# Four convolution-like layers on one core: query blocks of 10 rows in the attention layer, and three changes around it

## The chip, the core and the metric

The kernel runs on one core of a Trainium2 chip. The core has five engines with a queue of instructions each: TensorE (PE in the profile, with its weight loads as PEld), VectorE (DVE), ScalarE (ACT), GpSimd (POOL) and SyncE (SP, which here only issues DMAs). An engine takes its own instructions in the order in which they stand, and waits on semaphores for what other engines make. Data lie in SBUF (128 partitions), sums of matmuls in PSUM (eight banks), the rest in DRAM. The metric is the device time of one execution in microseconds (us); lower is better.

## What is computed

Four layers run one after the other on 4 images of 256 channels and 48 x 48 points, each as x = x + layer(norm(x)), all in float32. Layer 0 is a dilated 7 x 7 convolution whose softmax weights mix shifted copies of x. Layer 1 is a 3 x 3 convolution with signs for weights, layer 2 a 3 x 3 convolution with ternary weights (their size compared with 0.7 of its mean). Layer 3 is a linear attention with three windows, cut to what matters:

```python
q = sigmoid(Wq x); k = sigmoid(Wk x); v = Wv x / |Wv x|     # 8 heads of 32 channels
for w in (1, 2, 4):                # window of 48, 24, 12 points a side
    wkv  = box(integral(k v^T))    # sum over the window around each point
    wk   = box(integral(k))
    outs.append((q . wkv) / (q . wk + 1e-6))
x = x + Wout concat(outs) + bout
```

The kernel computes layer 3 in another order: scores q.k for all pairs of points within the widest window, times a mask of 0 and 1 for each window, times v.

## The kernel before

**Layers 0 to 2** (up to line 1440) run image by image. For image b the order on the queues is `attend(b)` (softmax and mixing of layer 0), `layer1`, `layer2`, `prelude(b + 2)`. Matmuls of the next image's convolution, `conv0(b + 1)`, are a *filler*: a generator from which `fill(us)` draws pieces where TensorE would otherwise wait. A second generator, `side`, prepares the weights of layers 1 and 2 once, during image 0: each `fill` also takes one step of it, and what is left after `attend(0)` is drained at lines 1430 and 1431, one step per `fill(1)`. `prepare_layer1` (line 577) loads a group of weights, takes signs on ScalarE, stores them; `prepare_layer2` (line 595) sums sizes with 18 matmuls (`abs_ps`), then for six groups loads again, takes size and sign on ScalarE, compares on VectorE (`kept`) and sums with 72 thin matmuls (`sum_ps`). For the last image the filler is `project_first` (line 1406), which makes q, k and v of image 0 in 12 groups for layer 3.

**Layer 3** (from line 1442) goes through blocks `(b, ct, rb)`: image, half of the channels (4 heads), query rows. A block before has 8 rows (RB, 384 points), so 6 to an image, 48 in all. Keys come in tiles of 8 rows by 16 columns: (a, c), with a from 0 to 5 and c from 0 to 2. Per tile:

- `scores` (1656): TensorE makes s = k.q for 4 heads in two pairs, a pair to a PSUM tile of two banks. The pool holds two such tiles, so one key tile fills it.
- `masked` (1674): `full` (1715) tells whether the widest window covers the middle columns for the whole block. If so, ScalarE copies these columns, and VectorE multiplies only the edges by the mask; if not, VectorE multiplies everything (`widest`). If the narrowest window is seen too (`many`), VectorE also makes the middle window from PSUM (`middle`), and GpSimd the narrowest from SBUF.
- `sums` (1767): TensorE multiplies by v into three accumulators, two tiles later (LAG = 2). So the order on TensorE is s(n), sums(n-2), s(n+1), sums(n-1).

`tiles_of` (1789) sets tiles with the narrow window (here *near*) and the others in alternation. The others are *ring* tiles (full, but not near) and *far* tiles (not full).

After each tile `advance()` takes a step of the jobs in the background: `Projection` of the next image (one part every two steps), `k_sums` (1491) and `norms` (1533) in a chain, which make the denominators on VectorE and GpSimd, and `finish` (1830), which divides and applies Wout (`out_ps`). A job's `yield n` puts its next step n tiles later; FETCH is 4. `until(key)` takes steps on the spot until something is made. `norms` loads `nhi` and `nlo` for both halves at once, then takes difference and product for one half after the other on GpSimd, sums on TensorE (`norm_ps`) and stores reciprocals (`r_d`). `prepare` (1803) loads them spread over partitions (`rc`). Keys and values have 12 buffers each (`kvp`, line 1445), and `LOADS` (1887) says after which block which key rows of the next half are loaded. All layer 3 loads go over SP's queue, at the start too: four pairs of key and value tiles, then q (lines 1881 to 1884). The masks come over GpSimd's queue (line 1458).

Most instructions carry line 142, that of the helper which records them; so they are told apart by the names of their tiles.

Of the kernel before, what the change touches and what calls it, by code (L numbers as in the profile page):

```python
# [21 lines left out]
P = 128  # L22
B, C, H, W = 4, 256, 48, 48
HW = H * W
# [56 lines left out]
NKT = NRB * NKC  # L81

# [63 lines left out]
def conv_preact_kernel(  # L146
# [76 lines left out]
    o_d = [dram.tile([NRB, P, NW * NB], F32, tag=f"o{b}", name=f"o_d{b}") for b in range(B)]  # L223
    n_d = [dram.tile([NRB, HEADS, NW, NB], F32, tag=f"n{b}", name=f"n_d{b}") for b in range(B)]
    r_d = [dram.tile([NRB, HEADS, NW, NB], F32, tag=f"r{b}", name=f"r_d{b}") for b in range(B)]
# [61 lines left out]
    class Projection:  # L287
# [6 lines left out]

        def ps_tile(self):
            t = self.psum.tile(self.shape, F32, tag=self.tag, name="proj_ps")
            return t if len(self.shape) == 2 else t[:, 0]

        def load(self, g, a, n):

            b = self.b
            yield from take("xr")
            xr = self.scr.tile([P, NCT, RB, W], F32, tag="xr", name="xr")
            sync.dma_start(
                out=xr,
                in_=x3_d[b][:, a * RB : (a + 1) * RB, :].rearrange(
                    "(ct p) r w -> p ct r w", p=P
                ),
            )
            yield FETCH  # L310
            yield from take("xn")
            xn = self.scr.tile([P, NCT, NKC, P], F32, tag="xn", name="xn")
            for ct in range(NCT):
                dve.tensor_scalar(
                    xn[:, ct].rearrange("p c (r x) -> p c r x", x=KC),
                    xr[:, ct].rearrange("p r (c x) -> p c r x", x=KC),
                    st3[:, b, 0, ct : ct + 1],
                    st3[:, b, 1, ct : ct + 1],
                    ALU.subtract,
                    ALU.mult,  # L320
                )
                yield 1
            free["xr"] += 1
            self.xn[g], self.uses[g] = xn, n
# [7 lines left out]
        def qk(self, g, a, name, mo):  # L332
            b = self.b
            while g not in self.xn:
                yield 1
# [29 lines left out]
        def v(self, g, a, c):  # L365
            b = self.b
            while g not in self.xn or (c > 0 and g not in self.vs):
                yield 1
# [74 lines left out]
    with (  # L443
# [133 lines left out]
        def prepare_layer1():  # L577
            for ct in range(NCT):
                for g in range(T1 // 3):
                    raw = new_wl().rearrange("p a o -> p (a o)")[:, 0 : 3 * C]  # L580
                    raw = raw.rearrange("p (t o) -> p t o", t=3)
                    sync.dma_start(out=raw, in_=wl1[ct * P : (ct + 1) * P, 3 * g : 3 * g + 3, :])
                    signs = new_wl().bitcast(BF16).rearrange("p a o -> p (a o)")[:, 0 : 3 * C]
                    signs = signs.rearrange("p (t o) -> p t o", t=3)
                    act.activation(signs, raw, AF.Sign)
                    for mo in range(NCT):
                        sync.dma_start(
                            out=wl1_d[mo, :, ct, 3 * g : 3 * g + 3, :],
                            in_=signs[:, :, mo * P : (mo + 1) * P],
                        )  # L590
                    yield
# [3 lines left out]
        def prepare_layer2():  # L595
# [14 lines left out]
            loaded = [load_raw(*groups[0])]  # L610
            for i, (ct, g) in enumerate(groups):
                if i + 1 < len(groups):
                    loaded.append(load_raw(*groups[i + 1]))
# [3 lines left out]
                for t in range(3):  # L617
# [6 lines left out]
                    )  # L624
            delta = smx.tile([P, 1, C], F32, tag="delta", name="delta", bufs=1)
# [10 lines left out]
            for i, (ct, g) in enumerate(groups):  # L636
                both = new_wl().rearrange("p (a t) o -> p a (t o)", a=2)
                both = both.rearrange("p a (t o) -> p a t o", t=3)
                signs, size = both[:, 0], both[:, 1]
                kept = new()  # L640
                sync.dma_start(out=signs, in_=wl2[ct * P : (ct + 1) * P, 3 * g : 3 * g + 3, :])
                rows.append(both)
                yield
# [7 lines left out]
                for what, src in ((0, size), (1, kept)):  # L651
                    for mo in range(NCT):
                        for t in range(3):
# [3 lines left out]
                                ones[:, 0:1],  # L657
# [367 lines left out]
        def apply0(xt, k, rows_at_hand, load_next, xTs):  # L1025
# [24 lines left out]
            for f in range(NPH):  # L1050
                now = seen
# [135 lines left out]
        def layer2(b, stats):  # L1187
# [70 lines left out]
            for h in range(thirds):  # L1258
                for mo in range(NCT):
                    for at in range(N2):  # L1260
                        ps = ps_cv.tile([P, R2, W], F32, tag="cv3", name="cv3")
# [130 lines left out]
        with (  # L1392
# [13 lines left out]
            def project_first():  # L1406
# [10 lines left out]
                start(paced(Projection(0, scr, ps, "ps", [P, 512]).groups(groups), 1))  # L1417
# [4 lines left out]
            for b in range(B):  # L1422
                if b + 1 < B:
                    filler = conv0(b + 1, {})
                else:
                    ending.close()
                    wts3 = ctx.enter_context(tc.tile_pool(name="wts_qkv", bufs=1, side="right"))
                    filler = project_first()
                stats = attend(b)
                for _ in side:  # L1430
                    fill(1)
# [11 lines left out]
    with (  # L1443
        tc.tile_pool(name="wts3", bufs=1, reuse_waits="tile") as wts,
        tc.tile_pool(name="kvp", bufs=2 * NRB, reuse_waits="tile") as kvp,
# [12 lines left out]
        masks = wts.tile([P, NMASK], BF16, name="masks")  # L1458
        nc.gpsimd.dma_start(out=masks, in_=masks_in[:, 0:NMASK])
# [9 lines left out]
        zeros = wts.tile([P, NB], BF16, name="zeros")  # L1469
# [63 lines left out]
        def norms(b, rb):  # L1533
# [4 lines left out]
            def load(ct):  # L1538
                chans = slice(ct * P, (ct + 1) * P)
                hi = scr.tile([P, NW, RB, W], F32, tag="nhi", name="nhi")  # L1540
                lo = scr.tile([P, NW, RB, W], F32, tag="nlo", name="nlo")
# [5 lines left out]
                for wi, h in enumerate(HALVES):  # L1547
# [7 lines left out]
                    if n < RB:  # L1555
# [3 lines left out]
                        )  # L1559

                    y0 = rb * RB - h - 1
# [5 lines left out]
                return hi, lo, qf  # L1567
# [5 lines left out]
            loaded = [load(ct) for ct in range(NCT)]  # L1573
            yield FETCH
            for hi, lo, qf in loaded:
                for wi, h in enumerate(HALVES):
                    n = min(RB, max(0, h + 1 - rb * RB))
                    if n < RB:
                        pool.tensor_sub(hi[:, wi, n:RB], hi[:, wi, n:RB], lo[:, wi, n:RB])
                yield 1  # L1580
# [22 lines left out]
            nn = HEADS * NW * NB // P  # L1603
            nr = scr.tile([P, nn], F32, tag="nr", name="nr")
            flat = [d[b][rb].rearrange("h w n -> (h w n)") for d in (n_d, r_d)]
            sync.dma_start(out=nr, in_=flat[0].rearrange("(p n) -> p n", n=nn))
# [4 lines left out]
            sync.dma_start(out=flat[1].rearrange("(p n) -> p n", n=nn), in_=nr)  # L1611
# [13 lines left out]
        def load_q(b, ct, rb):  # L1625
            qs = qp.tile([P, RB, W], F32, tag="qs", name="qs")
            sync.dma_start(
                out=qs.rearrange("p r w -> p (r w)"),
                in_=q_d[b][ct * P : (ct + 1) * P, rb * NB : (rb + 1) * NB],
# [3 lines left out]
        def rows_seen(wi, a, rb):  # L1633

            h = HALVES[wi]
            return (
                max(0, a * RB - h + 1 - rb * RB),
                min(RB, a * RB + RB + h - rb * RB),
            )
# [5 lines left out]
        class Block:  # L1645


            def __init__(self, b, ct, rb, qs):
# [5 lines left out]
                self.accs = self.stage = None  # L1654

# [18 lines left out]
            def masked(self, a, c, ss):  # L1674
# [8 lines left out]
                            [P, 2, RB, min(W, KC + 2 * HALVES[wi])],  # L1683
# [15 lines left out]
                def times_mask(engine, wi, rows, cols, dst, src):  # L1699
                    mr = rb * RB + rows[0] - (a * RB - HALVES[wi] + 1)  # L1700
# [14 lines left out]
                full = abs(a - rb) * RB + RB <= HALVES[0]  # L1715
# [42 lines left out]
            def begin(self):  # L1758
                self.accs = [
                    ps_acc.tile([P, NB], F32, tag=f"acc{i}", name=f"acc{i}") for i in range(NW)  # L1760
                ]
                self.stage = op.tile([P, NW, NB], F32, tag="stage", name="stage")

                for acc in self.accs[1:]:
                    pe.matmul(acc, zeros[:, 0:P], zeros, start=True, stop=False)
# [23 lines left out]
        def tiles_of(rb):  # L1789
# [4 lines left out]
                for a in sorted(range(NRB), key=lambda a: abs(a - rb))  # L1794
# [8 lines left out]
        def prepare(i):  # L1803

            b, ct, rb = order[i]
            yield from wait_for(("norm", b, rb))
            yield from take("o")
            o = op.tile([P, NW, NB], F32, tag="o", name="o", bufs=1)
            sync.dma_start(out=o.rearrange("p w n -> p (w n)"), in_=o_d[b][rb])
            yield from take("res")  # L1810
            res = scr.tile([P, NCT, RB, W], F32, tag="res", name="res")
            sync.dma_start(
                out=res,
                in_=x3_d[b][:, rb * RB : (rb + 1) * RB, :].rearrange("(ct p) r w -> p ct r w", p=P),
            )
            rcs = []
            for t in range(NCT):
                yield from take("rc")
                rc = op.tile([P, NW, NB], F32, tag="rc", name="rc")
                for g in range(HG):  # L1820
                    sync.dma_start(
                        out=rc[g * D : (g + 1) * D].rearrange("p w n -> p (w n)"),
                        in_=r_d[b][rb, t * HG + g]
                        .rearrange("w n -> (w n)")
                        .partition_broadcast(D),
# [4 lines left out]
        def finish(i, stage):  # L1830


            b, ct, rb = order[i]
            yield 1
            if ct == 0:
                sync.dma_start(out=o_d[b][rb], in_=stage.rearrange("p w n -> p (w n)"))
# [11 lines left out]
            for mo in range(NCT):  # L1848
                yield from bank(2)
                ps = ps_m.tile([P, 512], F32, tag="st", name="out_ps")[:, 0:NB]  # L1850
# [18 lines left out]
                out=out[b, :, rb * RB : (rb + 1) * RB, :].rearrange("(ct p) r w -> p ct r w", p=P),  # L1869
# [4 lines left out]
        order = [(b, ct, rb) for b in range(B) for ct in range(NCT) for rb in range(NRB)]  # L1874
        bank_m = ps_m, "st", [P, 512]

        for mo in range(NCT):
# [3 lines left out]
        seen_first = HALVES[0] // RB + 1  # L1881
        for a in range(seen_first):
            load_kv(0, 0, a)
        qs = {0: load_q(*order[0])}


        LOADS = {2: (0,), 3: (1, 2), 4: (3, 4), 5: (5,)}
# [20 lines left out]
        def midway(i):  # L1908

            b, ct, rb = order[i]  # L1910
            if (b, ct) == (0, 0) and 0 < rb <= NRB - seen_first:
                a = seen_first - 1 + rb
                until(("k", 0, 0, a), ("v", 0, a))
                load_kv(0, 0, a)
            if ct == NCT - 1:
                start(prepare(i))
            if i + 1 < len(order):
                nb, nct, nrb = order[i + 1]
                until(("q", nb, nct, nrb))
# [88 lines left out]
```

## Time and profile before

| | |
|---|---|
| median of 3 runs | 3803.53 us (3793.98, 3803.53, 3810.6) |
| profiled execution | 3796.91 us, span 3795.1 us |
| mean granted TensorE clock | 0.951 |
| layer 3, first scores to end | 1443.27 to 3795.1 us |
| busy share of the span: PE, DVE, ACT, POOL | 86%, 66%, 27%, 40% |

The busy times are unions over a whole span of unlike stages. A matmul that waits in the middle of a group (its second pair of heads waits for a bank) makes the group look busy for longer. So layer 3 is better read by the *pitch*, the time from the first scores matmul of one tile to that of the next in TensorE's timeline. The 720 pitches, summed over the eight halves of images, in us:

| | first half of the channels | second half |
|---|---|---|
| image 0 | 298.3 | 317.8 |
| image 1 | 328.7 | 285.0 |
| image 2 | 295.8 | 284.6 |
| image 3 | 244.7 | 272.1 |

Every half has the same 90 tiles; they differ in what runs beside them.

### The profile page before, as it was taken

Reading aid. Unit: us, or ns where it says so; the run is one execution under the profiler, and the core shown is the slowest. Engines: PE = TensorE matmul, PEld = TensorE weight load, DVE = VectorE, ACT = ScalarE, POOL = GpSimd, SP = SyncE. Lnnn points to the kernel's source line nnn. Section 1 sums busy time; section 2 is a strip of 40 time slices with the busy share of each in tenths; the row PEclk is TensorE's granted clock in tenths of the full one; section 3 lists DMA queues with packets and bytes.
Section 4 is the critical chain, followed back from the end, with each engine's and each line's share of the span. In section 5 each row is a group of like instructions: output and inputs, shape, how many; then the busy total and the mean of one; then the engine's idle time right before and its main releaser. Section 6 shows DMA issues by size and latency. Waiting matters only on the chain. (4 is left out here: it accounts for less than half of the span.)

```text
span 3795.1 us, 68918 instructions
## 1 busy us (share of the span) xinstructions
PE 3272.3 (86%) x26534; PEld 1886.4 (50%) x26534; DVE 2487.1 (66%) x5119; ACT 1034.1 (27%) x2024; POOL 1512.9 (40%) x2183
## 2 busy tenths in 40 slices
PE   3678898998997787988889789899999899989998
PEld 2457686786785673433334334344444344443443
DVE  7875488487484366777666567756577765655665
ACT  0012111111113323433222333332244332233331
POOL 0000030030030024778765486756365766344432
PEclk9798899999998898999999899999999999999999
DMA  7744324324323323345434243433223434101122
GB/s 250 235 132 143 117 89 125 108 94 125 105 70 118 115 76 114 122 131 167 118 109 130 83 138 126 151 108 108 76 97 113 147 106 123 50 31 50 45 60 59
DMA packets 373019, 423.04 MB, mean 111 GB/s; under 512 B 129076, under 2 KB 328532, under 8 KB 371540
## 3 DMA queue, kind: packets, MB, share of 16 engines
q1 hardware_dynamic: 371491, 416.32, 35.5%
q8 instruction: 211, 3.46, 0.4%
q0 software_dynamic: 144, 1.52, 0.2%
q14 instruction: 117, 0.95, 0.1%
q10 hardware_dynamic: 1056, 0.79, 0.1%
HBM read 288.79 MB, written 131.25 MB: 111 GB/s over the span
## 5 line engine op out<-in xcount | busy, mean ns | idle before, releaser
L142 DVE TENSOR_TENSOR sm<-s,masks 128x112 f32<-128x112 f32 (+10 forms) x2592 | 1135.0, 492 | 779.1 <-PE s L142 333.9
L142 POOL TENSOR_TENSOR sm<-sm,masks 128x432 f32<-128x432 f32 (+14 forms) x1152 | 851.9, 753 | 944.0 <-ACT sm L142 705.2
L142 PE MATMUL s<-qs,ks 32*128 32x320 f32 (+3 forms) x5760 | 834.5, 502 | 210.6 <-DVE sm L142 153.9
L142 ACT COPY sm<-s 128x528 f32<-128x528 f32 (+2 forms) x1152 | 594.2, 534 | 1483.5 <-PE s L142 1196.3
L142 PE MATMUL acc<-sm,vs 128*32 128x384 f32 (+18 forms) x13440 | 878.7, 385 | 12.9 <-POOL sm L142 12.7
L142 PEld LDWEIGHTS s<-qs,ks 32*128 32x128 f32 x5760 | 376.1, 186 | 617.7 <-DVE sm L142 240.4
L142 PE MATMUL cv<-vx,wt 128*128 128x288 f32 x2080 | 563.7, 427 | 90.4 <-DVE vx L142 50.3
L142 PEld LDWEIGHTS acc<-sm,vs 128*32 128x32 f32 x13440 | 354.9, 110 | 548.6 <-issue 350.8
L142 PEld LDWEIGHTS cv<-vx,wt 128*128 128x128 f32 x2080 | 405.5, 199 | 212.5 <-issue 50.7
L142 POOL MEMSET v<- 128x16 f32 (+1 forms) x120 | 18.5, 215 | 762.3 <-DVE vx L142 438.1
L142 PE MATMUL cv<-v,wl 128*128 128x384 f32 x1152 | 225.9, 356 | 23.2 <-DVE x L142 12.8
L142 PEld LDWEIGHTS cv<-v,wl 128*128 128x128 f32 x1152 | 216.2, 196 | 32.8 <-issue 16.2
L142 POOL TENSOR_TENSOR pt<-pt 128x144 f32<-128x144 f32 x336 | 186.6, 555 | 22.8 <-DVE pt L142 0.5
L142 POOL TENSOR_TENSOR v<-l2v,v 128x384 fp32r<-128x384 f32 x96 | 107.7, 1151 | 125.0 <-ACT v L142 124.9
L142 POOL TENSOR_TENSOR nhi<-nhi,nq 128x384 f32<-128x384 f32 x144 | 147.5, 1051 | 0.0
L142 PE MATMUL cv<-pad,wl 128*128 128x384 bf16 x864 | 143.1, 327 | 0.0
L142 PE MATMUL out_ps<-o,wout_sb 128*128 128x384 f32 x288 | 122.6, 508 | 10.5 <-DVE o L142 6.5
L142 POOL TENSOR_TENSOR sq<-vt 128x256 f32<-128x256 f32 x72 | 48.8, 680 | 201.9 <-ACT vt L142 171.7
L142 PE MATMUL out_ps<-stage,wout_sb 128*128 128x384 f32 x288 | 117.3, 489 | 0.0
L142 DVE TENSOR_TENSOR vx<-v 128x868 f32<-128x868 f32 x112 | 115.2, 1054 | 0.8 <-DVE v L142 0.5
L142 PEld LDWEIGHTS <-wl 128*128 128x128 bf16 x864 | 83.8, 97 | 59.1 <-issue 0.2
L142 DVE SCALAR_TENSOR_TENSOR x<-cv,alpha,x 128x384 f32<-128x384 f32 x144 | 83.9, 610 | 42.5 <-PE cv L142 42.1
(158 smaller groups left out, 2924.2 us busy)
## 6 DMA issues: line engine op xcount, KB each, us to landing
wt<-wt SPq DMA_DIRECT2D x48, 768.0 KB
kb_d<-pt SPq DMA_DIRECT2D x48, 576.0 KB
rc<-r_d SPq DMA_DIRECT2D x192, 144.0 KB
nhi<-kb_d SPq DMA_DIRECT2D x120, 192.0 KB
nlo<-kb_d SPq DMA_DIRECT2D x88, 192.0 KB
o_d<-stage SPq DMA_DIRECT2D x24, 576.0 KB
o<-o_d SPq DMA_DIRECT2D x24, 576.0 KB
wl<-wl_d SPq DMA_DIRECT2D x16, 768.0 KB
```

What stands on the lines that cost most here:

```text
L142: return lambda *args, **kwargs: self.tc.keep_in_program_order(op(*args, **kwargs))
```

## The change

Five things change; the diff is cut to them.

1. Layer 3's query blocks have 10 rows: blocks of 10, 10, 10, 10 and 8 rows, 40 blocks in all. Keys stay in tiles of 8 rows. `full` is written for any block. q, o, res, rc and the accumulators grow to 480 points; `r_d` is laid out by head over the whole image, so the reciprocals of one `norms` go out in eight DMAs. `LOADS` is one block earlier.
2. Key and value buffers: NRB + 3 = 9 of each. q is loaded ahead of the first keys.
3. `norms` loads `nlo` for one half at a time from one buffer, with a wait of FETCH steps ahead of the second half.
4. `prepare_layer1` and `prepare_layer2` load one or two groups ahead; `kept` and its column of ones become bf16 outside the weight pool; `apply0` takes a step of `side` in its inner loop; the drain is `fill(1.5)`.
5. In `layer2` of the last image the filler is drawn from between the matmuls, and from there on `project_first` takes no new group: what is left would start with layer 3 (`left`). The masks are loaded at the start of the last image.

```diff
+QR = 10
+QROWS = [(y, min(H, y + QR)) for y in range(0, H, QR)]
+NQB = len(QROWS)
+QN = QR * W
...
             yield from take("xr")
+            if self.enough:
+                free["xr"] += 1
+                self.left.append(g)
+                return
...
+            loaded = [load(*groups[0])]
+            yield
+            for i, (ct, g) in enumerate(groups):
+                if i + 1 < len(groups):
+                    loaded.append(load(*groups[i + 1]))
...
-            loaded = [load_raw(*groups[0])]
+            loaded = [load_raw(*group) for group in groups[:2]]
+            yield
...
-                kept = new()
-                sync.dma_start(out=signs, in_=wl2[ct * P : (ct + 1) * P, 3 * g : 3 * g + 3, :])
+                kept = smx.tile([P, 3, C], BF16, tag="kept", name="kept", bufs=1)
...
             for f in range(NPH):
+                if f > 0:
+                    next(side, None)
...
+                if b == B - 1 and h == 0:
+                    proj["first"][0].enough = True
                 for mo in range(NCT):
                     for at in range(N2):
+                        if b == B - 1:
+                            fill(1.2)
...
                 for _ in side:
-                    fill(1)
+                    fill(1.5)
...
-        tc.tile_pool(name="kvp", bufs=2 * NRB, reuse_waits="tile") as kvp,
+        tc.tile_pool(name="kvp", bufs=NRB + 3, reuse_waits="tile") as kvp,
...
             loaded = [load(ct) for ct in range(NCT)]
+            lo = load_less(0)
             yield FETCH
-            for hi, lo, qf in loaded:
+            for ct, (hi, qf) in enumerate(loaded):
+                if ct > 0:
+                    yield FETCH
...
+                if ct + 1 < NCT:
+                    lo = load_less(ct + 1)
                 yield 1
...
-            sync.dma_start(out=flat[1].rearrange("(p n) -> p n", n=nn), in_=nr)
+            for h in range(HEADS):
+                sync.dma_start(
+                    out=r_d[b][h, :, rb * NB : (rb + 1) * NB].rearrange("w (s n) -> w s n", n=nn),
+                    in_=nr[h * NW * 4 : (h + 1) * NW * 4],
+                )
...
             h = HALVES[wi]
-            return (
-                max(0, a * RB - h + 1 - rb * RB),
-                min(RB, a * RB + RB + h - rb * RB),
-            )
+            y0, y1 = QROWS[rb]
+            return max(0, a * RB - h + 1 - y0), min(y1, a * RB + RB + h) - y0
...
-                full = abs(a - rb) * RB + RB <= HALVES[0]
+                full = self.y1 - 1 - HALVES[0] <= a * RB and a * RB + RB <= self.y0 + HALVES[0]
...
-            yield from wait_for(("norm", b, rb))
+            yield from wait_for(("norm", b, (y1 - 1) // RB))
...
+        left = [groups[g] for g in made_first.left]
+        if left:
+            start(paced(Projection(0, scr, *bank_m).groups(left), 1))
...
+        qs = {0: load_q(*order[0])}
         for a in range(seen_first):
             load_kv(0, 0, a)
-        qs = {0: load_q(*order[0])}
-        LOADS = {2: (0,), 3: (1, 2), 4: (3, 4), 5: (5,)}
+        LOADS = {1: (0,), 2: (1, 2), 3: (3, 4), 4: (5,)}
```

## Prediction

> **What bounds the kernel now.** I read the page's first part, then busy times by half image, then layer 3's timeline tile by tile, then the longest waits outside layer 3. 2352 of 3795 us are layer 3. Two stretches of it, one crowded and one quiet (columns: PE, PEld, DVE, ACT and POOL busy us with instruction counts, clock, DMA share, GB/s):
>
> ```profile
> 1742.00:2059.00 317.00, 273.31 (x2616) 121.54 (x2608) 205.10 (x425) 86.79 (x175) 210.00 (x286) 0.95 0.45 128
> 3253.00:3498.00 245.00, 220.48 (x2442) 100.88 (x2438) 147.58 (x335) 81.13 (x162) 102.34 (x144) 0.99 0.13 40
> ```
>
> TensorE looks 90% busy even where nothing runs beside the tiles. The timeline there tells more: a near tile, a far one, the next near one.
>
> ```profile
> 3409.24 1.29 PE L142 MATMUL s<-qs,ks 32*128 32x384 f32 x8
> 3410.47 1.33 PE L142 MATMUL acc<-sm,vs 128*32 128x216 f32 x24
> 3410.66 2.28 DVE L142 TENSOR_TENSOR sm<-s,masks 128x624 f32<-128x624 f32 x6 [1.09 <-PE s L142]
> 3412.70 1.29 PE L142 MATMUL s<-qs,ks 32*128 32x384 f32 x8 [0.91 <-DVE sm L142]
> 3413.71 1.82 DVE L142 TENSOR_TENSOR sm<-s,masks 128x768 f32<-128x768 f32 x2 [0.78 <-POOL sm L142]
> 3414.74 1.65 PE L142 MATMUL s<-qs,ks 32*128 32x320 f32 x8
> ```
>
> VectorE waits for s, then s waits for VectorE to free its bank: pitch 3412.70 - 3409.24 = 3.46 us, of which the sums fill 1.33. So the bare loop is a chain s, DVE, s; TensorE's other work (projections, `out_ps`, `norm_ps`) comes on top. Image 3's halves show it: 272.1 with ten groups of `out_ps`, 244.7 with two.
>
> In the crowded stretch GpSimd is 66% busy and TensorE stands behind it, first for a mask, then inside `norm_ps`:
>
> ```profile
> 1794.05 3.46 POOL L142 TENSOR_TENSOR nhi<-nhi,nlo 128x336 f32<-128x336 f32 x3
> 1797.48 1.98 POOL L142 TENSOR_TENSOR sm<-sm,masks 128x352 f32<-128x352 f32 x2
> 1798.69 1.32 PE L142 MATMUL acc<-sm,vs 128*32 128x176 f32 x6 [3.34 <-POOL sm L142]
> ```
>
> Outside layer 3 these waits bear on the change:
>
> ```profile
> 273.83 0.65 PE L142 MATMUL trx<-ident,pad 128*120 128x128 f32 x4 [3.73 <-ACT xT L142]
> 291.57 2.90 PE L142 MATMUL abs_ps<-wl,ones 128*128 128x256 f32 x6 [10.24 <-ACT wl L142]
> 378.68 0.52 PE L142 MATMUL tra<-ident,rows 120*120 120x120 f32 x3 [2.18 <-ACT seen L142]
> 405.32 5.28 PE L142 MATMUL sum_ps<-ones,wl 128*128 128x1 f32 x24 [6.11 <-DVE wl L142]
> 425.62 5.28 PE L142 MATMUL sum_ps<-ones,wl 128*128 128x1 f32 x24 [4.21 <-DVE wl L142]
> 1443.27 1.66 PE L142 MATMUL s<-qs,ks 32*128 32x384 f32 x8 [10.30 <-DMA qs<-q_d]
> ```
>
> [...] means of 263 ns at 112, 618 at 448, 802 at 624 and 952 at 768 elements, about 145 + 1.05 N. [...] Here four heads' scores at 320 columns take 0.75 us start to start when both banks are free (1489.54 to 1490.30), but about 1.5 us when the second pair must wait (3414.74 to 3416.33): the two pairs then run one after the other. [...] the trace has a prefix sum on VectorE at 7.92 us (mean 1.14) while GpSimd works on `nhi`.
>
> **Part 1, blocks of 10 rows.** From the rule in `full` and the rows seen: a half image has 90 tiles now, 48 near, 24 ring, 18 far. Changed it has 81: 45 near (39 of 10 rows, 6 of 8), 9 ring, 27 far, of which nine see only 1 to 3 rows. Score columns are the same in sum, so the gain is fixed parts; against it, VectorE's mask elements grow from 851,968 to 935,296 (10%), since a taller block is less often full. Their 2592 instructions become 2304: by 145 + 1.05 N, 1270 to 1316 us, +46 in sum. ScalarE's and GpSimd's parts shrink.
>
> Sum of the chain for one half, pitches (median) from the quiet half, columns 1, 0, 2:
> - before: near 3.46 + 3.23 + 2.93 = 9.62, ring 2.27 + 1.91 + 1.89 = 6.07, far 2.02 + 1.71 + 1.71 = 5.44. 16 x 9.62 + 8 x 6.07 + 6 x 5.44 = 235.1 (measured 244.7, less two `out_ps` groups at 3.8 each: 237.1).
> - a near tile of 10 rows: VectorE's two middle masks grow by 112 to 164 elements, the edges by some 60: 0.30 us (0.39 in column 1). Scores: 1.7 ns a column (0.75 us at 320, 0.86 at 384), 80 to 96 columns, once or twice by how far the pairs overlap: 0.14 to 0.33. I take 0.51, 0.51 and 0.63: 9.62 becomes 11.27, or 17% for 25% more rows.
> - ring: scores 0.14, copy 0.12, edges 0.07: 7.0 for three. Far: full 8 rows 5.6; 0.15 a row (7 rows 1.63, 8 rows 1.78): 6.5 at 10 rows, 6.1 at 9, 3.1 at 3, 2.7 at 2, 3.5 for the three of 1 row, which stand without near tiles between.
> - after: near 13 x 11.27 + 2 x 9.62 - 2.4 (six rows that the middle window misses, 0.4 each) = 163.3; ring 2 x 7.0 + 6.1 = 20.1; far 4 x 6.5 + 6.1 + 5.6 + 3.1 + 2.7 + 3.5 = 47.0. In sum 230.4. Near tiles without a partner (9.13 for three, not 9.62) are 4 of 15 instead of 4 of 16 and longer: about 3 less.
>
> So 5 to 10 us a half; I take 7.5, -60 for eight. Bounds: if pitches grow by the full 25%, +20; if by 14% only, -100. TensorE's background work is the same in columns (`out_ps` 40 blocks x 480 or 384 columns for 48 x 384) and I count it unchanged.
>
> **Parts 2 and 3.** The nine buffers cost nothing on the path: the keys that must wait for a buffer are loaded a block (30 us or more) ahead of use. SP issues 192 stores of reciprocals instead of 24, at about 0.45 us each +76 us over 2300 us of a queue that is seldom full: hidden. The extra FETCH matters more. The halves with both `k_sums` and `norms` beside them are long: (0, second) has 318 = 237 + ten `out_ps` at 3.4 + three projection parts at 1.3 + 43, with six norms: 7 us each; (1, first) leaves 28 for four, 7 each. In (1, second) five norms cost 8 us. A norm is four bursts of 3.4 us on GpSimd in four tiles; the change puts four tiles between the halves. I take 10 norms beside `k_sums` from 7 to about 3.5 us and give 8 us back for image 0's last norms: they now come after their block, and its `finish` then waits for `rc`. -27; bounds -50 and +10.
>
> **Part 4.** The waits shown sum to 3.73 + 10.24 + 2.18 + 6.11 + 4.21 = 26.5 us, all behind a weight group that was loaded too late. bf16 for half of `sum_ps` saves about 5. In return `apply0` gets ScalarE steps of 1.72 us (size and sign) ahead of its `seen` copies: some six times 1.5 us. -20; bounds -32 and -5.
>
> **Part 5.** In the built programs, projection matmuls ahead of layer 3 are equally many, and in layer 3 both have 108 + 72 + 72, which is images 1 to 3 alone. So `left` is empty: nothing of image 0 moves into layer 3. One q projection moves ahead of layer 2, and q's load no longer stands behind the keys and the last stores: -6 of the 10.3 us; bounds -9 and 0.
>
> **Sum.** -60 - 27 - 20 - 6 = -113 on the span of 3795.1; the median lies 8.4 above this span, so 3803.5 - 113 = 3690.
>
> **Rivals.**
> - *A, as summed*, 3690, with its bounds about 3625 to 3750: 0.62.
> - *B, chain in proportion*: pitches grow 25% since the pairs of heads stay serial: +20 - 10 - 15 - 6, 3793. For it: +46 us of masks on VectorE. Against: the fixed parts seen. 0.15.
> - *C, fixed parts larger*: growth 14% and stalls gone: -100 - 50 - 30 - 8, 3615. For it: TensorE fills between. Against: the near tiles' serial pairs. 0.14.
> - *D, slower: the norms fall behind*. A norm takes about 21 steps for 17, in images of 162 steps for 180. Where it comes after its block, `finish` runs straight after the DMA issue and VectorE's queue, masks included, stands for ten issues (4.5 us) and the landing (5.37 in the chain that ended last). If all 15 finishes of images 0 to 2 did, +149: 3839. It decides from 12 finishes on. Against: in TensorE's order only image 0's come late. 0.09.
> - *That part 5 does nothing* is in every case.
>
> **Numbers.** A measurement tells about 0.5% (19 us). Faster: A, C and a third of B, 0.84; same 0.06; slower 0.10. Range 3600 to 3770: A whole, most of C.
>
> **What would show it.** Quiet half near 230; near pitch of 10 rows about 4.1, 3.7, 3.4; image 0's second and image 1's first half 20 or more shorter; no wait over 3 us at `abs_ps` and `sum_ps`; first scores near 1415. It is wrong if the quiet half exceeds 240, or DVE waits for `rc` in most finishes.

## The result: slower by 0.8%, and the profile after

The changed kernel takes 3834.18 us (median of four runs, 3827.95 to 3837.92) where the kernel before takes 3802.6 beside it: ratio 1.0082, 95% interval 1.0056 to 1.0108. The forecast was 3690 with a range of 3600 to 3770 and a chance of 0.10 for slower. Sign and size are wrong, and so is the quiet half: 243.5 us, where over 240 was named as a sign of being wrong.

The profiled execution has a span of 3833.9 us for 3795.1. Layer 3 begins 11 us earlier and lasts 50 us longer. By half images (first scores to first scores, the last one to the last scores, us):

| image, half | 0, 1st | 0, 2nd | 1, 1st | 1, 2nd | 2, 1st | 2, 2nd | 3, 1st | 3, 2nd |
|---|---|---|---|---|---|---|---|---|
| before | 298.3 | 317.8 | 328.7 | 285.0 | 295.8 | 284.6 | 244.7 | 272.1 |
| after | 289.8 | 343.3 | 304.9 | 304.8 | 303.5 | 310.4 | 243.5 | 276.2 |
| difference | -8.5 | +25.5 | -23.8 | +19.8 | +7.7 | +25.8 | -1.2 | +4.1 |

The same two stretches as in the prediction, the crowded one (image 0, second half) and the quiet one (image 3, first half), by busy times in a window, in the changed kernel (columns: PE, PEld, DVE, ACT and POOL busy us with instruction counts, clock, DMA share, GB/s); last, all of layer 3:

```profile
1722.00:2065.00 343.00, 276.73 (x2298) 111.12 (x2296) 221.62 (x398) 82.21 (x142) 199.65 (x266) 0.91 0.39 110
...
3289.00:3532.00 243.00, 217.16 (x2170) 90.14 (x2168) 156.10 (x302) 72.87 (x125) 110.97 (x138) 0.99 0.23 66
...
1432.00:3834.00 2402.00, 2080.34 (x18248) 855.50 (x18248) 1602.74 (x2975) 703.18 (x1225) 1238.19 (x1646) 0.94 0.34 100
```

Layer 3 of the kernel before, in the same view:

```profile
1443.00:3795.00 2352.00, 2087.41 (x20664) 946.93 (x20664) 1548.85 (x3288) 772.80 (x1536) 1360.57 (x1886) 0.97 0.34 101
```

TensorE is busy for as long as before (2080 us for 2087) with 12% fewer instructions; VectorE has 54 us more, as the prediction counted for its masks (46, by a fit to the means of VectorE's products in the trace before: 263 ns at 112 elements, 618 at 448, 802 at 624, 952 at 768). What is new is the clock, 0.94 for 0.97, and time in which no engine works. The waits of layer 3 name it. All waits on transfers over 1 us after the change (columns: us in all, times, longest):

```profile
DVE o L146 <- DMA rc<-r_d: 46.1, 4, 18.6
...
ACT sg L146 <- DMA q_d<-sg: 21.8, 4, 8.9
...
POOL nhi L146 <- DMA nlo<-kb_d: 20.1, 6, 6.7
...
DVE cs L146 <- DMA kp<-kf_d: 14.2, 3, 10.7
...
ACT vt L146 <- DMA v_d<-vt: 8.1, 1, 8.1
...
PE out_ps L146 <- DMA rc<-r_d: 5.7, 1, 5.7
```

and before:

```profile
PE s L142 <- DMA qs<-q_d: 10.3, 1, 10.3
...
DVE o L142 <- DMA rc<-r_d: 6.2, 1, 6.2
...
ACT sg L142 <- DMA q_d<-sg: 4.7, 1, 4.7
...
DVE cs L142 <- DMA kp<-kf_d: 3.9, 1, 3.9
```

The longest of them, in the timeline of the changed kernel (start, duration; in brackets the idle time before and what ended it):

```profile
2003.81 0.75 DVE L146 RECIPROCAL nr<-nr 96x96 f32<-96x96 f32 x1
...
2004.59 5.74 SPq L146 DMA_DIRECT2D r_d<-nr  x8
...
2010.89 2.36 SPq L146 DMA_DIRECT2D nhi<-kb_d  x4
...
2013.92 2.67 SPq L146 DMA_DIRECT2D nhi<-kb_d  x4
...
2016.63 2.43 SPq L146 DMA_DIRECT2D nlo<-kb_d  x3
2019.16 0.38 SPq L146 DMA_DIRECT2D o<-o_d  x1
2019.58 0.43 SPq L146 DMA_DIRECT2D res<-x_d  x1
2020.05 9.44 SPq L146 DMA_DIRECT2D rc<-r_d  x8
...
2032.54 0.66 DVE L146 TENSOR_TENSOR o<-o,rc 128x480 f32<-128x480 f32 x1 [18.58 <-DMA rc<-r_d]
...
2033.57 1.75 PE L146 MATMUL s<-qs,ks 32*128 32x320 f32 x8 [16.47 <-DVE sm L146]
```

Read it from the bottom. VectorE has come to `finish` of a block of image 0 and needs the reciprocals `rc`. Their norm was ready only at 2004.56 (the end of its reciprocal). SP then issues, in its queue's order, the eight stores of the reciprocals, the thirteen loads of the next norm (with two of `nq` not shown), and only then `o`, `res` and the eight loads of `rc`, at 1.18 us each where the median is 0.43. They land at 2032.5, 28 us after the reciprocal. The masks of the next tiles stand behind `o` in VectorE's queue, so scores stop for 16.5 us. Three windows of the changed kernel, in the stall and after it:

```profile
2018.00:2028.00 10.00, 0.00 (x0) 0.00 (x0) 0.00 (x0) 0.00 (x0) 0.00 (x0) 0.66 0.92 233
2033.00:2038.00 5.00, 4.43 (x36) 2.00 (x40) 4.29 (x9) 0.96 (x2) 4.40 (x5) 0.50 0.79 136
2042.00:2047.00 5.00, 4.03 (x44) 1.86 (x36) 4.91 (x10) 0.89 (x2) 4.46 (x6) 1.00 0.02 9
```

For ten microseconds no engine computes and the transfers run at 233 GB/s; when TensorE starts again, its clock is 0.50 for some 5 us, so the stall is in part paid a second time. All four waits of VectorE's `o` for `rc` end like this: the clock is 0.50 from 1954.1 to 1959.7, 2033.6 to 2038.2, 2113.3 to 2120.1 and 3817.4 to 3823.3 us, and 1.00 right after each. But the clock halved without so long a gap too, as "Why the prediction was wrong" shows under part 1, and the stalls explain the lower mean clock of layer 3 only in part: in e9 below, where the longest are gone, it is 0.96, with 8 rows (e10) 0.97.

Outside layer 3 the waits that part 4 was to remove are gone or small (after, timeline of TensorE):

```profile
289.20 1.53 PE L146 MATMUL abs_ps<-wl,ones 128*128 128x256 f32 x6 [1.95 <-ACT wl L146]
...
326.11 1.50 PE L146 MATMUL sum_ps<-ones,wl 128*128 128x1 f32 x12 [1.38 <-DVE wl L146]
```

and the first scores no longer wait for their queries:

```profile
1431.95 1.98 PE L146 MATMUL s<-qs,ks 32*128 32x480 f32 x8 [0.26 <-DMA ks<-k_d]
```

### The profile page after: what moved, and what is told of

Read it like the earlier page. It is cut to its first block, busy times and chain, and to the rows that moved or that the text cites. A ratio compares the mean times of both kernels' runs of the same rounds, so it can differ in the third digit from the quotient of the medians.

```text
span 3833.9 us, 62681 instructions
## 1 busy us (share of the span) xinstructions
PE 3270.4 (85%) x24082; PEld 1798.4 (47%) x24082; DVE 2542.6 (66%) x4799; ACT 965.4 (25%) x1713; POOL 1392.0 (36%) x1944
## 5 line engine op out<-in xcount | busy, mean ns | idle before, releaser
L146 DVE TENSOR_TENSOR sm<-s,masks 128x540 f32<-128x540 f32 (+20 forms) x2304 | 1190.2, 573 | 721.1 <-PE s L146 410.0
L146 POOL TENSOR_TENSOR sm<-sm,masks 128x540 f32<-128x540 f32 (+28 forms) x912 | 731.1, 812 | 1084.2 <-ACT sm L146 948.3
L146 PE MATMUL s<-qs,ks 32*128 32x400 f32 (+11 forms) x5184 | 826.7, 549 | 272.6 <-DVE sm L146 232.6
L146 PE MATMUL acc<-sm,vs 128*32 128x400 f32 (+25 forms) x11712 | 890.0, 428 | 6.7 <-POOL sm L146 6.7
L146 ACT COPY sm<-s 128x660 f32<-128x660 f32 (+5 forms) x864 | 520.8, 613 | 1441.3 <-PE s L146 1162.9
L146 PE MATMUL out_ps<-o,wout_sb 128*128 128x480 f32 (+1 forms) x240 | 118.0, 574 | 7.8 <-DMA rc<-r_d 5.7
L146 PE MATMUL proj_ps<-wv_sb,xn 128*128 128x256 f32 x288 | 88.6, 435 | 34.9 <-ACT vt L146 22.9
L146 PE MATMUL ap<-seen,xT 120*128 120x120 f32 (+3 forms) x832 | 117.5, 300 | 0.0
L146 PEld LDWEIGHTS ap<-seen,xT 120*128 120x128 f32 (+2 forms) x832 | 114.2, 218 | 0.1
L146 PE MATMUL out_ps<-stage,wout_sb 128*128 128x480 f32 (+1 forms) x240 | 113.9, 557 | 0.3 <-DVE stage L146 0.3
```

The costliest lines, as they stand in the source:

```text
L146: return lambda *args, **kwargs: self.tc.keep_in_program_order(op(*args, **kwargs))
```

## Experiments

What the order of the program says first, since the experiments build on it. Background work moves one step per key tile. A norm takes 16 steps before the change and 20 after, in images of 180 and 162 tiles. In image 0 the first norm can start at step 49 in both. Before, the six are ready at steps 65, 81, 97, 113, 129 and 145, and the blocks ask for them at 95, 107, 122, 140, 158 and 173: always in time. After, they are ready at 69, 89, 109, 129, 149 and 169, and the five blocks, which ask at 86, 101, 119, 137 and 155, need the norms ready at 89, 109, 129, 149 and 169: late by 3, 8, 10, 12 and 14 steps. In images 1 to 3 no block asks before its norm is there. Times are compared as ratios to the kernel before on the same chip.

| run | rows | stores of a norm | image 0's norms | us | ratio to before (95%) |
|---|---|---|---|---|---|
| changed kernel | 10 | 8 | late | 3834.2 | 1.0082 (1.0056 to 1.0108) |
| e1_short_norms | 10 | 8 | in time, all pauses short | 3834.5 | 1.0095 (1.0080 to 1.0110) |
| e2_one_store | 10 | 1 | late | 3795.0 | 0.9982 (0.9966 to 0.9999) |
| e3_rows8 | 8 | 8 | in time | 3798.6 | 0.9990 (0.9975 to 1.0006) |
| e4_weights_back | 10 | 8 | late | 3845.0 | 1.0120 (1.0087 to 1.0152) |
| e5_short_one | 10 | 1 | in time, all pauses short | 3790.1 | 0.9978 (0.9965 to 0.9991) |
| e6_rows8_one | 8 | 1 | in time | 3773.9 | 0.9937 (0.9912 to 0.9961) |
| e7_rows8_one_whole | 8 | 1, `nlo` not split | in time | 3785.6 | 0.9959 (0.9943 to 0.9974) |
| e8_weights_alone | 8 | as before | as before | 3788.3 | 0.9969 (0.9957 to 0.9981) |
| e9_rows10_head | 10 | 1 | in time | 3780.9 | 0.9967 (0.9953 to 0.9981) |
| e10_rows8_head | 8 | 1 | in time, earlier | 3781.5 | 0.9961 (0.9944 to 0.9977) |
| e11_rows8_kv12 | 8 | 1, twelve buffers | in time | 3780.4 | 0.9959 (0.9944 to 0.9974) |
| e12_head_eight | 10 | 8 | in time | 3802.8 | 1.0003 (0.9988 to 1.0018) |

**Shorter pauses in every norm.** In `norms`, three times:

```diff
-            yield FETCH
+            yield 2
```

> The changed kernel with the three pauses of a norm two steps long instead of four: a norm takes 14 steps for 20, all else is as changed. Lateness theory: the changed kernel lost its gain because the norms of image 0 are finished only 2 to 12 steps after the blocks that need them ask for them, so that `finish` stands in VectorE's queue for the reciprocals (46 us of waits for rc, 18.6 us the longest) and TensorE's clock falls after each such gap. Then the waits for rc fall under 12 us, image 0's second half goes from 343 to about 315, image 1's first from 305 to about 290, and the time falls by 30 to 50 us to about 3795. Chain theory (the taller tiles themselves and the work of norms and projections that moved into the second halves are the loss): waits move, the time stays within 12 us of 3834, and the halves of images 1 and 2 stay as long.

Measured 3834.5: the time of the chain theory, but with the lateness theory's sign, since the waits for `rc` did vanish. They went elsewhere (waits of this run):

```profile
POOL nhi L146 <- DMA nlo<-kb_d: 136.4, 24, 10.1
...
DVE o L146 <- DMA rc<-r_d: 9.8, 2, 5.3
```

GpSimd now reaches its subtraction before `nlo` has landed, and stands there with the masks behind it. Neither theory is shown by this; it says that SP's queue is long enough for a load issued two tiles ahead to come late.

**One store for eight.** At the end of `norms`:

```diff
-            for h in range(HEADS):
-                sync.dma_start(
-                    out=r_d[b][h, :, rb * NB : (rb + 1) * NB].rearrange("w (s n) -> w s n", n=nn),
-                    in_=nr[h * NW * 4 : (h + 1) * NW * 4],
-                )
+            sync.dma_start(
+                out=r_d[b][:, :, rb * NB : (rb + 1) * NB].rearrange("h w (s n) -> (h w) s n", n=nn),
+                in_=nr,
+            )
```

> The changed kernel with one store of a norm's reciprocals in place of eight; it writes the same numbers. Queue theory (SP's 168 more issues hold up the other transfers): waits on transfers in layer 3, 117 us now and 16 before the change, fall to under 60 us, and the time falls by 25 us or more. Lateness theory: the norms come as late as before, in step count nothing moves, so the waits for rc stay above 30 us and the time falls by 10 us at most.

The queue theory's numbers: 39 us faster, waits on transfers in layer 3 down from 117 to 47 us. The lateness is still there: VectorE's `o` still waits 30 us, 19.5 put down to `rc` and 10.2 to another transfer. The issues themselves, in the view of this tile in the changed kernel (ns: shortest, median, longest):

```profile
L146 SPq DMA_DIRECT2D r_d<-nr x192: 669/672/816, 1681.0 to 3430.8; - x192
L146 SPq DMA_DIRECT2D rc<-r_d x160: 302/432/1650, 1769.8 to 3813.4; - x160
```

and with one store:

```profile
L146 SPq DMA_DIRECT2D r_d<-nr x24: 763/779/872, 1673.6 to 3384.9; - x24
```

A store of 4.5 KB holds SP for 0.67 us, one of 36 KB for 0.78: the eight cost 5.4 us of SP for the same bytes. These spans are the time that SP was held, not that of the transfers: in the stall above SP was done with the last load of `rc` at 2029.49 and issued the next load, of `ks`, at 2030.05, while `rc` landed at 2032.5.

**Blocks of 8 rows in the changed kernel.**

```diff
-QR = 10
+QR = 8
-        LOADS = {1: (0,), 2: (1, 2), 3: (3, 4), 4: (5,)}
+        LOADS = {2: (0,), 3: (1, 2), 4: (3, 4), 5: (5,)}
```

> The changed kernel with blocks of 8 rows again (six per image, 180 tiles an image instead of 162), the rest as changed: split norms, eight stores, nine buffers, weights ahead. A norm still takes 20 steps, but the images have 18 steps more, and image 0's norms are then no more than one step late. Lateness theory: the chain's loss of about 60 us (7.5 us a half image) and the end of the late norms' stalls of about 45 us cancel, giving 3820 to 3850; the quiet half is about 252 (244.7 before, plus two norms at some 4), not 243.5. Chain theory (blocks of 10 rows lose by themselves): 3780 or less, with all second halves as before the change. My prediction's own step for part 1 stands if the quiet half is 7 us or more longer than 243.5.

3798.6, between the two: 36 us faster than with 10 rows. The quiet half lasts 245.5 us, within 2 us of the 243.5 at 10 rows: by the mark set beforehand, part 1 of the prediction falls.

**Weights prepared as before.** `prepare_layer1` and `prepare_layer2` of the kernel before, without the `next(side, None)` in `apply0`, and `fill(1)`.

> The changed kernel with the weights of layers 1 and 2 prepared as before the change (one load ahead at most, float32 ones for the counts, side steps only in the fills, fills of 1 instead of 1.5 at the end). Layer 3 begins at 1432 now and at 1443 before. If part 4 is worth the 20 us that the marks show before the last image's attention, and the 16 us lost in that attention come from the change's other parts (masks loaded there, fills in layer 2), layer 3 begins at about 1452 and the time rises by 20 us. If part 4 itself causes that later loss [...], layer 3 begins at about 1443 and the time rises by about 10 us.

Layer 3 begins at 1447.8, between the two; the time rises by 11 us, the second theory's number, with intervals that overlap. It decides nothing: the eleven profiles of kernels with the same layers 0 to 2 as the changed one begin layer 3 anywhere from 1415 to 1432.

**Short pauses and one store together.**

> The changed kernel with both edits tried alone so far: a norm's pauses two steps instead of four, and one store of its reciprocals instead of eight. Alone the first moved nothing (3834.5; the waits for rc fell from 46 to 10 us, but GpSimd waited 136 us for nlo), the second gave 39 us. If GpSimd's waits for nlo come from SP being held by the eight stores (0.67 us each, 5.4 us a norm), they fall under 60 us here, the waits for rc stay under 15 us, and the time is 3755 to 3775. If the pauses are simply shorter than a load takes, the waits for nlo stay over 90 us and the time is 3790 or more.

3790.1, with 59.4 us of GpSimd's waits for `nlo` and 4.8 of VectorE's `o` for `rc`: the waits are those of the first expectation, the time that of the second. Of e1's 136 us of waits for `nlo`, 77 came from the eight stores; the rest stays, since a pause of two steps is often too short for the load.

**8 rows and one store.** The edits of e2 and e3.

> The changed kernel with blocks of 8 rows and one store of a norm's reciprocals; compare with one store at 10 rows (3795.0) and eight stores at 8 rows (3798.6). If the stores hurt only where a block waits for its norm at once, as image 0's blocks of 10 rows do, they cost little at 8 rows: 3788 to 3799, and blocks of 10 rows are worth nothing either way once the stores are one. If a store costs every norm alike (39 us over 24 norms), the time is about 3760, and blocks of 10 rows lose some 35 us by themselves. My prediction's part 1 (60 us for 10 rows) would need 3855.

Ratio 0.9937; its neighbours with 8 rows and one store (e10, e11) have 0.9961 and 0.9959. The mean of the three, 0.9952, is 0.0038 (14 us) under e3: so stores cost something also where norms are in time. Both expectations missed: less than "every norm alike" (39 us), more than "little". e3 shows where it is paid: GpSimd waits 34.7 us for `nlo` there and 1.9 here, since the next norm's loads stand behind the stores.

**8 rows, one store, `nlo` whole.** Two `nlo` buffers, both loads at once, without the pause between:

```diff
-            lo = load_less(0)
+            los = [load_less(ct) for ct in range(NCT)]
             yield FETCH
             for ct, (hi, qf) in enumerate(loaded):
-                if ct > 0:
-                    yield FETCH
+                lo = los[ct]
```

> The changed kernel with blocks of 8 rows, one store of the reciprocals and both nlo loaded at once into two buffers, with no pause between: what is left of the change is the weights, the nine key buffers, the masks loaded in the last image and the reciprocals' layout. If the split costs or gives nothing in layer 3, layer 3 lasts 2352 us as before the change (within 8), and the time is 3780 to 3788. If spacing the norms out helps, as my prediction had it (27 us for the split), this is 20 us slower than the run with the split: about 3810.

3785.6, as the first expectation. The split moves time between halves (image 1's first half 327.9 whole, 313.2 split; image 2's first 295.7 whole, 311.9 split), and the sum by nothing that these runs can tell: 0.9959 whole, 0.9952 the mean of the three split ones.

**Part 4 alone in the kernel before.**

> The kernel before with part 4 alone: weights of layers 1 and 2 loaded ahead, bf16 for the counts, side steps between the steps of `apply0`. If my step for part 4 holds (20 us), layer 3 begins at about 1423 instead of 1443 and the time falls by 15 to 20 us to about 3785. If the loss in the last image's attention (16 us) is caused by part 4, layer 3 begins at 1436 or later and the time falls by less than 10 us.

Neither expectation as a whole: layer 3 begins at 1440.1, as the second has it (one profile, with the spread just named), but the time falls by 12 us (ratio 0.9969), more than the second's 10 and less than the first's 15. Up to the last image's attention, part 4 gives what was predicted (it begins at 1153.1 for 1175.9, and 1155.2 with the whole change). Then most of it is lost. That attention with the same number of matmuls, before, with part 4 alone, and in the changed kernel:

```profile
1175.90:1317.00 141.10, 101.07 (x485) 75.94 (x486) 56.33 (x161) 65.20 (x111) 11.61 (x22) 0.79 0.41 130
```

```profile
1153.10:1308.70 155.60, 108.82 (x485) 82.86 (x486) 56.61 (x161) 66.63 (x112) 12.05 (x22) 0.74 0.38 118
```

```profile
1155.20:1312.10 156.90, 109.91 (x485) 82.87 (x486) 56.68 (x161) 66.62 (x112) 11.81 (x22) 0.72 0.41 126
```

It takes 14 to 16 us longer at a clock of 0.72 to 0.74 for 0.79. In all twelve profiles with part 4 it lasts 150.6 to 159.0 us; in e4, which prepares the weights as before and keeps the rest of the change, 148.9. There is one profile of the kernel before, so how much of the loss is part 4's stays open. In program order a few of image 0's projection matmuls stand a step earlier or later between the transposes there, since the fills carry over another remainder. Whether this order makes the gaps, or the clock does, was not settled.

And with part 4 alone the first scores still wait for the queries:

```profile
1440.11 1.66 PE L142 MATMUL s<-qs,ks 32*128 32x384 f32 x8 [10.42 <-DMA qs<-q_d]
```

In the changed kernel that wait is 0.26 us, so its end is part 5's.

**10 rows, one store, image 0's norms early.** The edit of e2, and in `norms`, three times:

```diff
-            yield FETCH
+            yield 2 if b == 0 else FETCH
```

Image 0's norms are then ready at steps 63 to 133, each before its block asks.

> The changed kernel (blocks of 10 rows) with one store of the reciprocals, and the pauses of a norm two steps instead of four in image 0 alone, so that image 0's norms are ready before their blocks ask while the other images' norms keep their pauses. With one store alone the time was 3795.0 and image 0's second half 329.6 with 30 us of waits for rc. If late norms in image 0 are what is left of the loss of blocks of 10 rows against 8 (3773.9 with one store), image 0's second half goes to 312 or less, the waits for rc under 10 us, and the time is 3772 to 3782: then 10 rows are worth nothing in themselves. If 10 rows also gain in the chain (my part 1, 60 us), the time would fall under 3750. If the time stays at 3790 or more, lateness was not the cause of the rest.

3780.9, as the lateness theory had it; image 0's second half 314.7 for 329.6 with one store alone (312 or less was expected); the waits for `rc`:

```profile
DVE o L146 <- DMA rc<-r_d: 4.7, 1, 4.7
```

The one left is the last block's, which the kernel before has too.

**The same with 8 rows.**

> The same two edits with blocks of 8 rows. Its norms of image 0 are hardly late without the shorter pauses (a step at most), so the lateness theory expects no more than 6 us from 3773.9; a fall of 15 us or more would say that a norm's pauses cost something else than lateness.

Ratio 0.9961, no fall. Beside e9's 0.9967 it is the fair comparison of 10 rows with 8: 0.0006, or 2 us, where the intervals leave some 8 us either way.

**Twelve buffers.**

```diff
-        tc.tile_pool(name="kvp", bufs=NRB + 3, reuse_waits="tile") as kvp,
+        tc.tile_pool(name="kvp", bufs=2 * NRB, reuse_waits="tile") as kvp,
```

> Blocks of 8 rows, one store of the reciprocals, and twelve key and value buffers as before the change instead of nine. If nine buffers cost nothing on the path, as my prediction said, this is within 6 us of 3773.9; if a block ever waits for a buffer, it is 10 us or more faster.

0.9959: not faster. Nine buffers cost nothing that shows.

**10 rows, eight stores, image 0's norms early.** The edit of e9 in the changed kernel.

> The changed kernel (10 rows, eight stores of the reciprocals) with the pauses of a norm two steps instead of four in image 0 alone. It is the missing corner: eight stores and late 1.0082 of the time before, one store and late 0.9982, one store and not late 0.9967, this one eight stores and not late. If the stores hurt mainly because SP still holds the reciprocals' loads behind them when a late block's `finish` already waits, this is about 3800 (0.998 to 1.002) and the waits for rc are under 12 us. If each store costs the same wherever it stands, it is 0.9967 plus 0.010, about 3830.

1.0003, and 5.5 us of waits for `rc`: the first expectation. It closes a square at 10 rows: late and eight stores 1.0082, late and one 0.9982, in time and eight 1.0003, in time and one 0.9967. Eight stores cost 0.0100 (38 us) where norms are late and 0.0036 (14 us) where they are not; lateness costs 0.0079 (30 us) with eight stores and 0.0015 (6 us, within the intervals) with one. The two together make the 44 us between the changed kernel and e9. The 14 us in time are GpSimd's waits for `nlo` again: 48.5 us here, 9.4 in e9.

## Why the prediction was wrong

**Part 1, -60: failed.** Its sum for one half image was 235.1 before and 227.4 after. In the traces, pitches summed over image 3's blocks that have no `out_ps` beside them (the first block of its second half, all but the first of its first half), a half has 237.1 before and 237.9 in e1, where no norm runs beside these blocks. By kinds of tile:

| kind | predicted after, us a half | e1 |
|---|---|---|
| near | 160.3 | 166.2 |
| ring | 20.1 | 20.3 |
| far, 8 to 10 rows | 37.7 | 39.4 |
| far, 1 to 3 rows | 9.3 | 12.0 |

Three near tiles of 10 rows came out as priced (means 4.00, 3.80 and 3.48 us in columns 1, 0 and 2: 11.28; priced 11.27). The nine far tiles of 1 to 3 rows (*thin* tiles), which blocks of 10 rows bring, cost 1.3 us each, where 1.0 was taken: more than half of what a tile of 8 to 10 rows took (39.4 us for 18, 2.2 each). The two deductions, 2.4 us for rows that the middle window misses and 3 for near tiles without a partner, do not show in the sum of e1's near tiles. Together the misses exceed the whole gain of 7.5 us a half.

But one of these 45 near pitches lasts 7.13 us. TensorE runs at half clock there, behind three tiles of one row and a wait for VectorE (e1):

```profile
3343.00:3346.40 3.40, 1.44 (x18) 0.60 (x16) 2.22 (x6) 1.45 (x2) 1.31 (x2) 1.00 0.01 2
3346.40:3356.60 10.20, 9.26 (x46) 3.14 (x50) 5.08 (x10) 1.75 (x3) 3.15 (x3) 0.50 0.42 137
...
3346.83 2.41 PE L146 MATMUL s<-qs,ks 32*128 32x480 f32 x8 [2.27 <-DVE sm L146]
```

In e2 the same tile takes 3.45 us, at clock 1.00. Without this pitch the mean of column 0 is 3.52, and three near tiles take 11.0, less than their price. So some 3.7 of the 5.9 us by which the near tiles miss are the clock's, a term that the prediction put at nothing. It is not this tile alone. Summed over layer 3, the clock records of the seven profiles with 10 rows have 196 to 276 us at half clock, those of the seven with 8 rows 134 to 162 (e9 204, e10 138). They come in stretches of 3.4 us or a whole multiple of it (3.4 to 17.1 us in the changed kernel). In e9, 29 of 33 stretches, and in the changed kernel 35 of 42, begin with no gap as long as the shortest stretch between matmuls in the 6.8 us ahead of them. So TensorE had not stood still for that long there; in the changed kernel it had been busy for 29 to 81% of the 6.8 us ahead, where the mean of layer 3 is 87%. In e9, 18 of the 33 begin at a thin tile or within three tiles after one, where only 27% of the tiles stand. If TensorE set the pace throughout, e9's 66 us more at half clock would cost 33 us (an estimate from these records). That this is what ate the gain is argued: no run takes out the thin tiles alone. What the runs show is the sum: 10 rows give nothing, in e1's quiet blocks and, by e9 against e10, in the whole program.

**Parts 2 and 3, -27: failed, twice.** Image 1's first half did become 24 us shorter, as one of the marks asked, but image 0's second, which the same mark named, 25.5 longer; and where `nlo` is whole (e7) the time is what the split ones have. The gain in one half was taken for a gain of the sum. And "SP +76 us: hidden" was a costly step. The stores took 0.67 us each, not 0.45 (the loads of `rc` before: 0.42 at the median); and more than their sum counts that they come in a row of 5.4 us, ahead of loads that another engine is about to need. By e12 and e9 this is 14 us where the norms are in time, by the changed kernel and e2 38 where they are late.

**Part 4, -20, and part 5, -6.** Part 4's waits went as said, the six groups of `sum_ps` took 10.7 us of TensorE for 22.4 (the f32 half of a group 1.44 to 1.55, the bf16 half 0.29 or 0.30; before, 2.73 to 5.28 for both), and the last image's attention begins 20.7 us earlier; 15.8 of these are lost inside it, a loss that the prediction did not look for. Part 5 took away the wait of 10 us for the first queries; from the end of that attention to the first scores it is 119.9 us for 126.3, so 6.4 net, where 6 were forecast. With both, layer 3 begins at 1415 to 1432 in the eleven profiles of kernels that have them, median 1426: 17 us for the 26 predicted. That nothing of image 0 moves into layer 3 held.

**Rival D, 0.09, was the one.** It named the place (`finish` after its norm, VectorE's queue with the masks in it) and, by luck, nearly the total (3839), but not how it gets there: its 149 us were for 15 late finishes on top of all the gains, and the runs have three that wait and few of the gains. It priced a late finish at 4.5 us of issues and 5.4 of landing, and let it decide from 12 finishes on; against it stood that only image 0's come late. That is so: of image 0's five late norms three make `finish` wait, 24.7 us in its second half (two waits) and 16.2 us in image 1's first: 13.6 us each and not 9.9. What was left out is the order in SP's queue: the stores, then the next norm's loads, and then the loads that the late block waits for; and the half clock after the longest gaps.

So, from one measured step to the next, in us of 3800: weights, queries and buffers -16 (e7), split 0, eight stores +14 (e12 less e9), 10 rows +2 (e9 less e10), late norms with eight stores +30 (changed less e12): +30 in sum. (The steps lie on one path from the kernel before to the changed one, so that they meet the measured +31 is no check; each is good to some 8 us.) The prediction had -26, -27, 0, -60 and, inside the -27, 8 for late norms.

Two readings of the prediction do not hold either. Its chance of faster, 0.84, is more than the parts it names (0.62 + 0.14 + 0.05 = 0.81). And the prefix sum of 7.92 us beside GpSimd's work on `nhi` is one of 48: the other 45 that run beside GpSimd for a third of their time or more take at most 1.41, so the trace does not show that work on GpSimd slows VectorE's. No sum rests on it.

Kernels with the weights ahead, one store and blocks of 8 rows (e6, e10, e11) beat both: 0.9937 to 0.9961 of the time before.

## What to carry to other kernels

When a change shortens the loop in which background work is stepped, or lengthens a background job, count for each job the step at which it is ready and the step at which it is asked for; one that is late by a few steps puts its whole chain of transfers on the path. For a DMA queue the sum of issue times says little: look at what stands in a row ahead of the load that someone is waiting for, and write many small stores as one. In a sum of loop pitches, price the thin tiles that a new block size brings with what each keeps of a full one (1.3 of 2.2 us here), and look in the trace at which clock they and the tiles behind them run.

## What the runs showed of the hardware

- The issue of a store of reciprocals took 0.67 us for 4.5 KB on 12 partitions (changed kernel, median) and 0.78 for 36 KB on 96 (one store for eight, e2). In the kernel before, with another layout in DRAM, 36 KB took 0.32.
- A load of `rc` (144 or 180 KB) held SP for 0.43 us at the median, and for 1.18 where eight followed fifteen others while the DMA engines were 92% busy at 233 GB/s (changed kernel, 2018 to 2028 us).
- A gap of 16 us on TensorE was followed by some 5 us at half clock (changed kernel, 2033.6 to 2038.2 us). The clock also halved for 10 us after a gap of 2.3 us, where TensorE had been busy for 1.44 of 3.4 us (e1). The mean clock of layer 3 (0.97 before, 0.94 after, 0.96 in e9) counts both, gaps and slow work.
